# Cross-attention with a state-space scan: the last query block in two halves, the scan begun in the pipeline's drain and the last 256 steps scanned on their own

## The chip, the cores and the metric

The kernel runs on one core of a Trainium2 chip. Its engines are PE (TensorE: matmul, with weight loads shown as PEld), DVE (VectorE), ACT (ScalarE), POOL (GpSimd) and SP (SyncE, used here as the main DMA queue). The metric is the device time of one execution in microseconds; the median of the runs shown is 2639.42 us.

## The reference

`x` (4096 x 512) gives the queries and the residual, `ctx` (3202 x 512) the keys and values; there are 8 heads of 64, and the state has 64 entries.

```python
x = _layernorm(builder_state, g1, beta1)
base_n = _layernorm(base_state, g1, beta1)
x = residual + _mha(x, base_n, W_qkv, b_qkv, W_o, b_o)
residual = x
xn = _layernorm(x, g2, beta2)
U = (xn @ W_in.T + b_in) @ Bmat

def step(s, u_t):
    s = jax.nn.silu(s @ A.T) + u_t
    return (s, s)
_, states = jax.lax.scan(step, jnp.zeros((builder_state.shape[0], S), U.dtype), U.transpose(1, 0, 2))
ssm_out = jnp.einsum('tbs,sh->bth', states, Cmat)
x = residual + ssm_out
mod = program_probs.mean(axis=1) @ W_prog.T + b_prog
return x + mod[:, None, :]
```

The scan runs one step after another along the 4096 positions. The mean of a second context gives `mod`, one row for all. Everything is in f32.

## The kernel before

**Preparation (to about 300 us).** The context is normalised, transposed and projected; keys and values are written to DRAM (`kd`, `vd`) as 13 double chunks of up to 248 keys for each pair of heads. Constants are folded: `rowb` (the attention's output bias), `modb` (the program bias), `wc`, `bu`, and `a_t`, the transposed state matrix twice on a 128x128 diagonal, so that two halves of the sequence run on 128 partitions.

**The attention loop.** The 4096 queries are 8 blocks Q of 512. A unit is (Q, hp, half): one pair of heads and 256 queries; units run with `half` innermost, so one load of keys and values (`load_k`, `load_v`, four steps ahead, 13 buffers each) serves two units. A unit has 13 steps, one for each double chunk. The whole order is written out by hand: iteration g of one loop (L721) issues, for every engine, `running` of step g-1 (DVE maximum, L480), `weights` of step g-17 (ACT exp, L524, and POOL's accumulation `acc`, L533, a tile of 123x1024), `scores` of step g (PE, L459, and ACT's copy to SBUF, L469), `subtract` of step g-16 (DVE, L514) and `product` of step g-18 (PE, L542). The exact maximum of a unit is known only after all its scores (`maximum`), hence the distance of 16 steps; each engine carries out its own instructions in the order in which they are issued. After the last scores the loop goes on for 18 iterations with subtractions, exps and products alone: this is called the drain below. For the very last unit every second accumulation is done on PE instead (`sums`, L558).

One generator at a time is advanced beside the steps by `background`: `finish` (divides a unit's output by the sum of its weights), `queries` (normalises and projects the next block) and `project` (for each tile of 128 rows of a finished block: output projection L627, residual, second normalisation, transposes L136, then `u` through `wc`, L659 and L663, and the row itself to DRAM, `x1d`, L648). Tiles of the loop write x1 without `modb`; the adds of `modb` come later, as rows are fetched back (L784).

**After the loop (L768 on).** The pools are released. The four tiles of the last block run through `project` together, as the scheduler orders them; the rows of all blocks are fetched back from `x1d` in the scan's layout, row = (v, c, j): v one of two halves of the sequence (on partitions 0 to 63 and 64 to 127), c one of 128 chunks in it, j one of 16 positions in a chunk.

**The scan.** The recurrence forgets its start quickly, so 256 chunks of 16 steps run side by side: sweep a does the last 8 positions of each chunk from no state, sweep b all 16 from what a left in the chunk before, sweep c 16 more from b, with outputs. One step is a matmul with `a_half` on h (L853), a tanh (L857) and one DVE operation (L858, h = (tanh + 1) z); the matmul of `a_t` on u was put into the same PSUM bank ahead (L840, L845). `output` adds u (L864), multiplies by `c2` (L870, two matmuls of 512 columns), adds the row (L873) and writes it from ACT's queue (L874). A final check compares the ends of sweeps b and c within 2^-21; if one differs, a sequential loop under `tc.If` repeats the work (L905).

```python
            nc.scalar.activation(th, zj, AF.Tanh, scale=0.5)
            nc.vector.scalar_tensor_tensor(h[:, j, :], th, 1.0, zj, ALU.add, ALU.mult)
```

Of the kernel before, what the change touches and what calls it, by code (L numbers as in the profile page):

```python
# [31 lines left out]
WARM = 8  # L32
NCK = T // L // 2
# [12 lines left out]
def xattn_ssm_kernel(  # L46
# [30 lines left out]

    u = const.tile([P, L, NCK], F32, name="u")

# [159 lines left out]
    def side():  # L239
# [75 lines left out]
        yield  # L315
        mean = wp.tile([NS, 1], F32, name="mean")
# [116 lines left out]
    lctx = ExitStack()  # L433
# [132 lines left out]
    def finish_last(w):  # L566
        Q, hp, half = w["at"]
        o = o_t[Q, hp][:, half * QU : (half + 1) * QU]
        nc.scalar.copy(o, w["po"][:, 0, :])
        sums(w["pd"], w["acc"], CK, False, True)  # L570
        rd = op.tile([P, QU], F32, tag="rd", name="rd_last", bufs=1)
# [4 lines left out]
        nc.vector.tensor_tensor(o, o, rd, ALU.mult)  # L576

    def finish(w):
# [3 lines left out]
        if half == 0:  # L582
            o_t[Q, hp] = op.tile([P, QB], F32, tag="o", name=f"o_{Q}_{hp}")
        o = o_t[Q, hp][:, half * QU : (half + 1) * QU]
# [31 lines left out]
    def project(Q, tiles=range(NT), pools=None):  # L616

        xp, n_x, n_t = pools or (xp_, 3, 1)
        for t in tiles:
            r = Q * QB + t * P  # L620
            xt = xp.tile([P, H], F32, tag="x", name=f"xr_{r}", bufs=n_x)
# [4 lines left out]
            for c in range(NC):  # L626
                nc.tensor.matmul(  # L627
                    pa,
                    o_t[Q, c][:, t * P : (t + 1) * P],
# [5 lines left out]
            x1 = xp.tile([P, H], F32, tag="x1", name=f"x1_{r}")  # L635
            nc.vector.tensor_tensor(x1, pa, xt, ALU.add)  # L636
            scaled = normalize(x1, P, f"y{r}", later=True)
            xs = x1
            if Q == NQB - 1:

                nc.gpsimd.tensor_tensor(xt, x1, modb, ALU.add)
                xs = xt
# [5 lines left out]
            nc.sync.dma_start(x1d[r : r + P, :], xs)  # L648
            tp = transposes(ps_m, "m", xh, P, f"y{r}")
            yield True  # L650
            xn = xp.tile([P, NC, P], F32, tag="xn2", name=f"xn2_{r}", bufs=n_t)
# [6 lines left out]
            for c in range(NC):  # L658
# [8 lines left out]
                None,  # L667
                ALU.add,
            )
# [4 lines left out]
    def load_k(i, c):  # L674

        Q, hp, half = units[i]
        if half == 0:
            t = kp.tile([P, 2 * CK], F32, tag="k", name=f"k_{Q}_{hp}_{c}")
            n = 2 * keys(2 * c)
            nc.sync.dma_start(t[:, :n], kd[hp, c, :, :n])  # L680
            kts[Q, hp, c] = t

    def load_v(i, c):
        Q, hp, half = units[i]
        if half == 0:
            t = kp.tile([CK, 2, P], F32, tag="v", name=f"v_{Q}_{hp}_{c}")
# [5 lines left out]
    units = [(Q, hp, half) for Q in range(NQB) for hp in range(NC) for half in range(2)]  # L692
# [24 lines left out]

    with tc.manual_schedule():
        for g in range(AHEAD):
            load_k(*steps[g])  # L720
        for g in range(len(steps) + NDC + LAG + 2):  # L721
# [22 lines left out]
            if exp:  # L744
                weights(*exp)
            if now:
# [5 lines left out]
            if mul:  # L752
                product(*mul)
                if mul[0]["last"] and mul[1] == NDC - 1:
                    finish_last(mul[0])
# [42 lines left out]

# [163 lines left out]
```

## Time and profile before

| | us |
|---|---|
| median of 3 runs | 2639.42 |
| lowest and highest run | 2634.09, 2639.81 |
| profiled execution, its time | 2643.8 |
| its span | 2642.0 |
| busy in the span: PE, DVE, ACT, POOL | 2498.9, 2144.1, 1837.8, 2066.3 |
| mean granted PE clock | 0.981 |
| last running maximum starts | 2468.65 |
| last sum of weights ends on PE | 2498.75 |
| first matmul of sweep a | 2545.02 |
| sweep c's first state on DVE | 2583.71 |
| end of the span | 2642.0 |

The profile's rows give, for a group of instructions: start, busy time, engine, line, operation, output and inputs with their shapes and the count; in brackets, how long the engine had been idle and what ended that. Windows give the busy time of every engine between two points in time, the mean clock granted to PE, and what the DMA engines did. One execution is profiled, and its time is 4.4 us above the median of the runs.

### The profile page before, as it was taken

What the parts mean: (1) busy time and instruction counts of PE and PEld (TensorE: products, weight loads), DVE (VectorE), ACT (ScalarE), POOL (GpSimd) and SP (SyncE); (2) the same over time, 40 slices, a digit from 0 to 9 for tenths busy, and PEclk for the clock granted to TensorE, in tenths of its full rate; (3) what the DMA queues carried; (4) which work ended last, traced back from release to release, by engine and by line L of the source; (5) the groups of instructions that cost most, each with busy time, mean ns of one, the idle gap of its engine ahead of it and who ended that gap; (6) DMA issues with size and microseconds to landing.
All of it is one profiled execution on the core that took longest, in us unless ns stands there. A gap on an engine that the chain in (4) does not pass through costs nothing.

```text
span 2642.0 us, 44166 instructions
## 1 busy us (share of the span) xinstructions
PE 2498.9 (95%) x16588; PEld 1422.2 (54%) x16588; DVE 2144.1 (81%) x2320; ACT 1837.8 (70%) x2085; POOL 2066.3 (78%) x1170
## 2 busy tenths in 40 slices
PE   7989899999999999999999999999999999999857
PEld 3445456555565555555655555555655555555433
DVE  2210897999979897999799988999799979999725
ACT  2232787877878787878787777778787878788510
POOL 1020497998979997999799988989799979999860
PEclk9999999999999999999999999999999999999966
DMA  3422221112212121222112211222121312221133
GB/s 124 138 87 73 74 68 49 51 57 84 59 45 62 50 83 32 58 65 68 45 54 68 67 56 51 57 84 59 43 62 49 86 30 60 64 58 54 60 112 128
DMA packets 164458, 176.62 MB, mean 67 GB/s; under 512 B 13480, under 2 KB 137424, under 8 KB 164242
## 3 DMA queue, kind: packets, MB, share of 16 engines
q1 hardware_dynamic: 155070, 157.68, 20.6%
q10 hardware_dynamic: 9172, 16.06, 1.8%
q8 instruction: 134, 2.20, 0.4%
q14 instruction: 82, 0.67, 0.1%
HBM read 143.81 MB, written 29.89 MB: 66 GB/s over the span
## 4 chain that ended last, share of the span: by engine, by line
PE 50%; DVE 27%; issue 11%; ACT 7%; POOL 2%; DMA 1%; SPq 1%; ACTq 0%; DVEq 0%; POOLq 0%
DVE top L480 17%; PE s L459 14%; PE po L542 12%; DVE p L514 5%; PE pq L175 4%; ACT p L469 4%; PE pa L627 4%; PE pv L388 3%; PE pk L414 3%; ACT p L524 2%; PE tt L491 2%; PE py_c L870 1%; DVE rd L599 1%; PE mb L506 1%; PE pu L659 1%
## 5 line engine op out<-in xcount | busy, mean ns | idle before, releaser
L533 POOL TENSOR_TENSOR acc<-p,acc 123x1024 f32<-123x1024 f32 x698 | 1658.7, 2376 | 112.2 <-ACT p L524 70.6
L469 ACT COPY p<-s 123x1024 f32<-123x1024 f32 (+1 forms) x832 | 834.9, 1004 | 274.6 <-PE s L459 261.9
L514 DVE TENSOR_TENSOR p<-p,mb 123x1024 f32<-123x1024 f32 (+1 forms) x832 | 1000.0, 1209 | 0.8 <-PE mb L506 0.8
L459 PE MATMUL s<-q,k 64*123 64x256 f32 (+1 forms) x6656 | 941.4, 402 | 61.2 <-DVE top L480 49.4
L524 ACT ACTIVATE p<-p 123x1024 f32<-123x1024 f32 (+1 forms) x832 | 880.2, 1058 | 141.2 <-DVE p L514 134.0
L480 DVE TENSOR_TENSOR top<-s,top 123x1024 f32<-123x1024 f32 x704 | 855.9, 1216 | 140.1 <-ACT p L469 132.2
L542 PE MATMUL po<-p,v 123*64 123x256 f32 (+1 forms) x6656 | 900.4, 392 | 1.1 <-ACT o L585 0.9
L459 PEld LDWEIGHTS s<-q,k 64*123 64x123 f32 (+1 forms) x6656 | 560.2, 182 | 374.3 <-DVE top L480 169.3
L542 PEld LDWEIGHTS po<-p,v 123*64 123x64 f32 (+1 forms) x6656 | 404.4, 136 | 399.0 <-issue 222.5
L533 POOL TENSOR_TENSOR acc<-p,p 124x1024 f32<-124x1024 f32 x64 | 152.0, 2376 | 161.2 <-ACT p L524 161.0
L627 PE MATMUL pa<-wo,o 128*128 128x512 f32 x256 | 119.6, 612 | 2.5 <-DVE x L636 2.5
L115 POOL TENSOR_SCALAR ve_c<-mv_c 123x1 f32<-123x1 f32 (+1 forms) x26 | 5.9, 228 | 146.9 <-DVE mv_c L113 116.7
L175 PE MATMUL pq<-xn,wq 128*128 128x256 f32 x512 | 117.9, 383 | 0.0
L358 DVE COPY ct<-tp_c 128x492 f32<-128x492 f32 (+1 forms) x13 | 8.7, 671 | 127.8 <-PE tp_c L136 127.8
L480 DVE TENSOR_TENSOR top<-s,p 124x1024 f32<-124x1024 f32 x64 | 77.7, 1214 | 38.7 <-DMA k<-kd 37.4
L175 PEld LDWEIGHTS pq<-xn,wq 128*128 128x128 f32 x512 | 94.8, 190 | 20.5 <-issue 6.3
L388 PE MATMUL pv<-wv,ct 128*123 128x512 f32 (+1 forms) x208 | 97.8, 615 | 0.0
L422 ACT ACTIVATE ks<-pk,bias 128x492 f32<-128x492 f32 (+2 forms) x28 | 18.0, 643 | 111.8 <-PE pk L414 63.6
L414 PE MATMUL pk<-ct,wk 128*128 128x492 f32 (+2 forms) x224 | 89.2, 550 | 0.0
L588 POOL TENSOR_TENSOR both<-acc 124x512 f32<-124x512 f32 x63 | 80.8, 1283 | 4.9
L627 PEld LDWEIGHTS pa<-wo,o 128*128 128x128 f32 x256 | 46.8, 192 | 62.5 <-issue 56.5
L498 DVE TENSOR_REDUCE m<-tt 128x2 f32<-128x496 f32 x128 | 79.7, 662 | 0.7 <-PE tt L491 0.7
(158 smaller groups left out, 1345.5 us busy)
## 6 DMA issues: line engine op xcount, KB each, us to landing
k<-kd SPq DMA_DIRECT2D x352, 123.0 KB
v<-vd SPq DMA_DIRECT2D x352, 123.0 KB
xr<-in_x_dram SPq DMA_DIRECT2D x32, 256.0 KB
out_dram<-row_c ACTq DMA_DIRECT2D x32, 256.0 KB
k<-kd SPq DMA_DIRECT2D x64, 124.0 KB
v<-vd SPq DMA_DIRECT2D x64, 124.0 KB
x<-in_x_dram SPq DMA_DIRECT2D x28, 256.0 KB
x1d<-x SPq DMA_DIRECT2D x28, 256.0 KB
```

What stands on the lines that cost most here:

```text
L175: nc.tensor.matmul(pq[:, half * QU : (half + 1) * QU], wq[:, i, hp * P : (hp + 1) * P], xns[half][:, i, :], start=(i == 0), stop=(i == NC ...
L388: nc.tensor.matmul(pv[:n, :H], ct[:, i, o : o + n], wv[:, i, :], start=(i == 0), stop=(i == NC - 1),)
L414: nc.tensor.matmul(pk[:, :n_g], wk[:, i, hp * P : (hp + 1) * P], ct[:, i, :n_g], start=(i == 0), stop=(i == NC - 1),)
L459: nc.tensor.matmul(s[:n, a, b, :], kts[(*w["at"][:2], c)][r, b * n : (b + 1) * n], q[r], start=True, stop=True,)
L469: nc.scalar.copy(t[:n], s[:n])
L480: nc.vector.tensor_tensor(w["top"][:n], s[:n], before[:n], ALU.max)
L514: nc.vector.tensor_tensor(t[:n], t[:n], w["mb"][:n].unsqueeze(2).to_broadcast([n, 2, 2, QU]), ALU.subtract,)
L524: nc.scalar.activation(t[:n], t[:n], AF.Exp)
L533: nc.gpsimd.tensor_tensor(w["acc"][:n], t[:n], before[:n], ALU.add)
L542: nc.tensor.matmul(w["po"][a * HD : (a + 1) * HD, 0, :], vts[(*w["at"][:2], c)][:n, b, a * HD : (a + 1) * HD], t[:n, a, b, :], start=(c == ...
L588: nc.gpsimd.tensor_tensor(both, acc[:, :, 0, :], acc[:, :, 1, :], ALU.add)
L627: nc.tensor.matmul(pa, o_t[Q, c][:, t * P : (t + 1) * P], wo[:, c, :], start=(c == 0), stop=(c == NC - 1),)
```

## The change

Four things change.

1. **The last block by halves.** Its units run with `half` outermost: all four head pairs for queries 3584 to 3839, then all four for the last 256. Keys and values are loaded again for the second half. The first half's two tiles go through `project` in the loop's background.
2. **The row adds.** Every tile now gets `modb` on POOL in `project`, before it is written to `x1d`; the adds at the fetch are gone.
3. **The scan of the first 3840 positions** (`main_scan`) starts in the drain: 12 of its steps are issued in iterations 1 to 8, 10, 12, 14 and 16 after the last scores, between ACT's exp and DVE's subtraction. Its steps hold the state s = h + u instead of h, so that a step is one matmul, a tanh and two DVE operations, and nothing is put into PSUM ahead. Rows are fetched from SP's queue during the drain. The rest of the scan is issued alternately with the last two tiles and the small scan; of an output's two halves, one goes over ACT and POOL, the other over DVE, and both are written from SP's queue.
4. **The last 256 positions** (`last_rows`) have a scan of their own: two tiles on the two halves of the partitions, 16 chunks of 8 positions each, with 24 positions of warm-up and 8 of result, 32 steps in a row on 16 columns. A second check compares their starts.

`a_t` is halved and `u` is doubled; the columns of `u` that belong to the last 256 positions are zeroed.

```diff
+LT = 8
+PRE = 3 * LT
...
+    END = NCK - QU // L
+    nc.gpsimd.memset(u[NS:, :, END:], 0.0)
...
+        nc.vector.tensor_scalar(a_t, a_t, 0.5, None, ALU.mult)
...
     def finish_last(w):
         Q, hp, half = w["at"]
-        o = o_t[Q, hp][:, half * QU : (half + 1) * QU]
+        o = op.tile([P, QU], F32, tag="o", name=f"o_{Q}_{hp}_{half}", bufs=12)
+        o_t[Q, hp, half] = o
         nc.scalar.copy(o, w["po"][:, 0, :])
         sums(w["pd"], w["acc"], CK, False, True)
+        yield
...
-    def project(Q, tiles=range(NT), pools=None):
-        xp, n_x, n_t = pools or (xp_, 3, 1)
+    def project(Q, tiles=range(NT), wait=0):
+        for _ in range(wait):
+            yield False
...
-            xs = x1
-            if Q == NQB - 1:
-                nc.gpsimd.tensor_tensor(xt, x1, modb, ALU.add)
-                xs = xt
+            nc.gpsimd.tensor_tensor(xt, x1, modb, ALU.add)
...
-            nc.sync.dma_start(x1d[r : r + P, :], xs)
+            nc.sync.dma_start(x1d[r : r + P, :], xt)
...
     def load_k(i, c):
         Q, hp, half = units[i]
-        if half == 0:
-            t = kp.tile([P, 2 * CK], F32, tag="k", name=f"k_{Q}_{hp}_{c}")
+        if half == 0 or Q == NQB - 1:
+            t = kp.tile([P, 2 * CK], F32, tag="k", name=f"k_{Q}_{hp}_{half}_{c}")
...
-    units = [(Q, hp, half) for Q in range(NQB) for hp in range(NC) for half in range(2)]
+    units = [(Q, hp, half) for Q in range(NQB - 1) for hp in range(NC) for half in range(2)]
+    units += [(NQB - 1, hp, half) for half in range(2) for hp in range(NC)]
...
+    def fetch(j):
+        if j not in rows:
+            rows[j] = sp_.tile([P, 2, H], F32, tag="s", name=f"row_{j}")
+        for v, n in enumerate(counts):
+            nc.sync.dma_start(rows[j][:n, v, :], x1r[v, j, :n])
+    def last_fetch():
+        for g in range(2):
+            r = LAST + g * P
+            t = xp_.tile([P, H], F32, tag="x", name=f"xr_{r}", bufs=3)
+            nc.sync.dma_start(t, x[r : r + P, :])
+            xl.append(t)
...
+        for g in range(2):
+            nc.gpsimd.tensor_tensor(xl[g], xl[g], rowb, ALU.add)
+    def step(j, before, s, z):
+        nc.tensor.matmul(z, a_t, before, start=True, stop=True)
+        th, h = sv["th"][j % 2], sv["h"][j % 2]
+        nc.scalar.activation(th, z, AF.Tanh, scale=0.5)
+        nc.vector.scalar_tensor_tensor(h, th, 1.0, z, ALU.add, ALU.mult)
+        nc.vector.tensor_tensor(s, h, u[:, j, :], ALU.add)
...
+    def sweep(first, start, end):
+        before = start
+        for j in range(first, L):
+            s = end[:, 1:] if j == L - 1 else sv["s"][j % 3]
+            step(j, before, s, zs(j))
+            before = s
+            yield j, s
+        nc.vector.tensor_copy(end[NS:, 0:1], end[:NS, NCK : NCK + 1])
+    def products(j, s):
+        for v, n in enumerate(counts):
+            r = slice(v * NS, (v + 1) * NS)
+            nc.tensor.matmul(sv["py"][j % 2][v], s[r, :], sv["c2"][r], start=True, stop=True)
+    def outputs(j):
+        py, t, y = sv["py"][j % 2], rows[j], sv["y"][:, j % 2, :]
+        nc.scalar.activation(y, py[1], AF.Copy, scale=0.5)
+        nc.vector.scalar_tensor_tensor(
+            t[:, 0, :], py[0], 0.5, t[:, 0, :], ALU.mult, ALU.add
+        )
+        n = counts[1]
+        nc.gpsimd.tensor_tensor(t[:n, 1, :], y[:n], t[:n, 1, :], ALU.add)
+        for v, n in enumerate(counts):
+            nc.sync.dma_start(outr[v, j], t[:n, v, :]) if n == NCK else nc.sync.dma_start(
+                outr[v, j, :n], t[:n, v, :]
+            )
...
+    def main_scan():
+        ends = sv["end0"], sv["end1"]
+        sv["z"] = ps_s.tile([P, 2, 4, NCK], F32, tag="s", name="z")
+        for end in ends:
+            nc.vector.memset(end[:NS, 0:1], 0.0)
...
+        for _ in sweep(L - WARM, u[:, L - WARM - 1, :], ends[0]):
+            yield
+        for _ in sweep(0, ends[0][:, :NCK], ends[1]):
+            yield
+        for j, s in sweep(0, ends[1][:, :NCK], ends[0]):
+            yield
+            products(j, s)
+            outputs(j)
+            yield
+        differ(ends[0][:, 1:], ends[1][:, 1:], NCK, sv["bad"])
+        yield
+    def last_rows(w):
+        yield from finish_last(w)
+        Q, tiles = NQB - 1, range(2)
+        pas, x1s, scaled, xns = [], [], [], []
+        for g in tiles:
+            pa = ps_m.tile([P, H], F32, tag="m", name=f"pa_l{g}")
+            pas.append(pa)
+            for c in range(NC):
+                nc.tensor.matmul(
+                    pa, o_t[Q, c, 1][:, g * P : (g + 1) * P], wo[:, c, :],
+                    start=(c == 0), stop=(c == NC - 1),
+                )
+            yield
+        for g in tiles:
+            x1 = xp_.tile([P, H], F32, tag="x1", name=f"x1_l{g}")
+            x1s.append(x1)
+            nc.vector.tensor_tensor(x1, pas[g], xl[g], ALU.add)
+            scaled.append(normalize(x1, P, f"yl{g}", later=True))
+            yield
+        tps = []
+        for g in tiles:
+            xh = scaled[g]()
+            tps.append(transposes(ps_m, "m", xh, P, f"yl{g}"))
+            nc.gpsimd.tensor_tensor(xl[g], x1s[g], modb, ALU.add)
+            yield
...
+        for g in tiles:
+            xn = sv["xn"][:, g, :].rearrange("p (c k) -> p c k", c=NC)
+            nc.scalar.copy(xn, tps[g])
...
+        for i in range(PRE // LT + 1):
+            nc.tensor.matmul(
+                zl[:, i, :], a_t, ul[:, i * LT : i * LT + P], start=(i == 0), stop=True,
+                skip_group_check=True,
+            )
+        yield
+        before = None
+        for t in range(PRE + LT):
+            i, j = divmod(t, LT)
+            z = zl[:, i, j::LT]
+            if before is not None:
+                nc.tensor.matmul(z, a_t, before, start=False, stop=True, skip_group_check=True)
+            h = (hl if i == PRE // LT else hw)[:, j::LT]
+            nc.scalar.activation(th, z, AF.Tanh, scale=0.5)
+            nc.vector.scalar_tensor_tensor(h, th, 1.0, z, ALU.add, ALU.mult)
+            if t == PRE:
+                nc.vector.tensor_tensor(sv["st"], hw[:, LT - 1 :: LT], ul[:, PRE :: LT][:, : P // LT], ALU.add)
+            before = h
+            yield
+        nc.vector.tensor_tensor(sl[:, 1:], hl, ul[:, PRE + 1 :], ALU.add)
+    def last_outputs(name):
+        sl = sv["sl"]
+        for g in range(2):
+            hs = slice(g * NS, (g + 1) * NS)
+            py = ps_m.tile([P, H], F32, tag="m", name=f"py_{name}_{g}")
+            sv["pyl", g] = py
+            nc.tensor.matmul(py, sl[hs, 1:], sv["c2"][hs], start=True, stop=True)
+        for g, queue in enumerate((nc.sync, nc.scalar)):
+            nc.vector.scalar_tensor_tensor(
+                xl[g], sv["pyl", g], 0.5, xl[g], ALU.mult, ALU.add
+            )
+            queue.dma_start(out[LAST + g * P : LAST + (g + 1) * P, :], xl[g])
...
+    SCAN_AT = (*range(1, 9), 10, 12, 14, 16)
+    scan = main_scan()
...
+            k = g - len(steps)
+            if k == 0:
+                assert not rest
+                last_fetch()
+            if k in SCAN_AT:
+                next(scan)
...
-                if mul[0]["last"] and mul[1] == NDC - 1:
-                    finish_last(mul[0])
-                elif mul[1] == NDC - 1:
+                if mul[1] == NDC - 1 and not mul[0]["last"]:
                     first.append(finish(mul[0]))
-                    if mul[0]["at"][1:] == (NC - 1, 1):
+                    if mul[0]["at"] == (NQB - 1, NC - 1, 0):
+                        rest.append(project(NQB - 1, range(NT // 2), wait=8))
+                    elif mul[0]["at"][1:] == (NC - 1, 1):
                         rest.insert(0, project(mul[0]["at"][0]))
+            if 0 < k <= L:
+                fetch(k - 1)
...
-        while first or rest:
-            background()
-    lctx.close()
...
-    def fetch(v, j, c0, c1, name):
...
-    tails = [project(NQB - 1, (t,), (tp_, NT, NT)) for t in range(NT)]
-    for g in tails:
-        next(g)
-    for j in range(L):
-        fetch(0, j, 0, NCK, "c")
-        fetch(1, j, 0, done, "c")
-    while tails:
-        for g in list(tails):
-            if next(g, None) is None:
-                tails.remove(g)
-    for j in range(L):
-        fetch(1, j, done, NCK, "c")
...
+        end = last_rows(ws[len(units) - 1])
+        next(end)
+        for _ in end:
+            next(scan, None)
+        for _ in scan:
+            pass
+        last_outputs("a")
+        neighbours()
+        differ(sv["sl"][:, : P : LT], sv["st"], P // LT, sv["badl"])
...
```

## The prediction

> **What bounds the kernel now.** I read the stages first (busy time of each engine in windows), then the count of steps in the last block, the timeline of the tail, and the granted clock inside it. Columns after the window: length, then busy PE, PEld, DVE, ACT, POOL with counts, clock, DMA share, GB/s.
>
> ```profile
> 2468.65:2498.75 30.10, 24.64 (x213) 15.10 (x211) 22.20 (x28) 18.62 (x20) 27.05 (x12) 1.00 0.01 2
> 2498.75:2545.02 46.27, 25.41 (x80) 14.35 (x80) 10.26 (x20) 5.48 (x8) 42.53 (x44) 0.74 0.80 231
> 2545.02:2582.67 37.65, 25.00 (x68) 13.99 (x69) 9.11 (x29) 6.66 (x24) 10.69 (x9) 0.70 0.01 2
> 2582.67:2636.40 53.73, 46.92 (x99) 19.09 (x97) 31.06 (x70) 4.44 (x16) 0.00 (x0) 0.61 0.39 147
> 2636.40:2642.00 5.60, 0.19 (x2) 0.09 (x2) 1.63 (x8) 0.00 (x0) 0.00 (x0) 0.68 0.29 102
> ```
> From the last running maximum on, 173.35 us: drain 30.1, four last tiles 46.3, sweeps a and b 37.7, sweep c with outputs 53.7, end 5.6. No engine is full there except PE in sweep c; they are chains. Before it, the block's loop, by windows of ACT's copies of scores (one per step) and of all engines:
>
> ```profile
> 2158.00:2250.00 92.00, 39.01 (x39) 1.00 0.20 56
> 2250.00:2346.00 96.00, 33.82 (x34) 1.00 0.25 73
> 2346.00:2466.00 120.00, 50.19 (x51) 1.00 0.15 42
> ...
> 2250.00:2346.00 96.00, 96.00 (x666) 54.33 (x664) 88.20 (x94) 72.80 (x81) 86.20 (x50) 1.00 0.25 73
> 2346.00:2466.00 120.00, 115.87 (x882) 65.82 (x880) 119.08 (x118) 100.96 (x109) 115.00 (x52) 1.00 0.15 42
> ```
> A plain step costs 212/90 = 2.36 us, and DVE is full (119.08 of 120); with four tiles of a projection inside, PE is full and 34 steps take 96 us, so a tile costs (96 - 34 x 2.36)/4 = 4.0 us. POOL has 9.8 us spare there.
>
> **The change, part by part.** What is removed is the whole of the stages after the drain (143.25 us); what replaces it is summed below, stage by stage. The zeroing of u's end and the halving of a_t are one short instruction each beside the first 300 us of preparation: nothing.
>
> Loop. Two tiles move into it: +8.0. Their POOL adds of modb, and those of the 28 earlier tiles, are new there: 30 x 1.265 us. Below, 0 (POOL has 9.8 us spare per four tiles for 5.1); above, all 38. I take 2: DVE has waited for POOL's rowb add, 16.8 us over 18 tiles, so cover is not complete. The write of a tile to DRAM now waits for that add; behind it on SP stand key and value loads, some nine steps (21 us) early, so 4 us later hurts nobody. Reloaded keys and values (104 DMAs of 123 KB) run at the rate that every second unit has now; their buffers are free nine (keys) and seven (values) steps before. Nothing; without that cover, the landing of a load per step. Sum +10.
>
> Drain. It gets twelve scan steps. Order matters: in an iteration ACT runs exp, then the scan's tanh; DVE runs the scan's two operations, then the next subtraction; that exp waits for the subtraction before it. So these iterations are one ring: subtraction 1.21 + exp 1.06 + tanh 0.28 + 2 x 0.29 + four hand-overs of 0.03 = 3.25 us, where DVE now needs 1.21. PE's products stand behind a scan matmul that waits for DVE, but within the ring. First three iterations: 7.8 us to the first subtraction of the last unit, plus three shortened rings, 11.4. That holds the scan's setup copies too. Then five rings 16.3, one bare 1.2, three (ring + bare) 13.4, reduction and reciprocal 1.2, last exp, product and sums 3.0: 46.5. The 32 row loads now stand on SP among the value loads: 7.9 MB in some 50 us (158 GB/s; 311 were moved between 2500 and 2520). Each waits for a buffer that the product one step before frees, and the value loads behind have five steps to spare: nothing, or one step's 3.25 us if a load came late.
>
> The step's last operation adds two SBUF tensors, and POOL is adding accumulators beside it (27.05 of 30.1 us). The trace has no such DVE operation beside POOL; it has copies of 128x127:
>
> ```profile
> 2536.11 19.60 POOL L784 TENSOR_TENSOR row_c<-row_c,modb 128x512 f32<-128x512 f32 x16
> 2545.00 1.01 DVE L820 COPY us<-u 128x127 f32<-128x127 f32 x1
> 2555.12 0.67 DVE L828 COPY he<-h 128x127 f32<-128x127 f32 x1
> 2580.72 0.23 DVE L828 COPY he<-h 128x127 f32<-128x127 f32 x1
> ```
> 0.23 us without POOL; with it the second copy ends 0.08 us after POOL's last add (2555.71). So it waited for the running add. Bounds per step: 0 (the subtraction with one SBUF input runs at 1.21 beside POOL throughout) and one whole accumulator add, 2.38. I follow the copies: half an add, 1.2. POOL's work here, 27.05 + 2 x 1.27 for the rows, fills 0.6 of 50 us: 12 x 0.6 x 1.2 = 8.6. Drain 55.1, between 46.5 and 75.
>
> The Trainium skill (SBUF — State Buffer, Who interferes with whom) speaks against the change here: a VectorE tensor-tensor with both inputs in SBUF contends with GpSimd's reads, and whichever comes second is blocked for the whole instruction. By the page the sum is as above; if only copies were blocked, it would be 8.6 less, and no run here shows the tensor-tensor yet.
>
> Last two tiles. Ten scan steps run between them in program order. At full clock: reciprocals and scaling 2.5; two projections (1.85 + scan matmul 0.5) 4.7; twice add, statistics and the scan's DVE pair (1.56 + 0.62) 4.4; twice normalise 0.81, transposes 0.66, scan matmul to its end 1.45: 5.8; twice copy 0.59, four matmuls 1.0, scan 1.45: 6.1; u and the four matmuls of the small scan 2.6; 26. At half clock behind the projections about 32. Taken: 30.
>
> Scan steps and outputs. The rows for a step, at both clocks:
>
> ```profile
> 2549.20 0.49 PE L853 MATMUL z_a<-h,a_half 128*128 128x128 f32 x2 [0.69 <-DVE h L858]
> 2549.72 0.28 ACT L857 ACTIVATE th_a<-z_a 128x128 f32<-128x128 f32 x1 [0.90 <-PE z_a L853]
> 2550.03 0.29 DVE L858 SCALAR_TENSOR_TENSOR h<-th_a,z_a 128x128 f32<-128x128 f32 x1 [0.89 <-ACT th_a L857]
> ...
> 2584.78 4.93 PE L870 MATMUL py_c<-c,st_c 64*128 64x512 f32 x8
> ...
> 2604.82 3.10 PE L870 MATMUL py_c<-c,st_c 64*128 64x512 f32 x8
> ```
> A step now takes 1.17 us (1.48 at half clock); the added DVE operation makes it 1.5 (1.8). The first two small steps go beside two of these: 2 x (1.8 + 0.35) = 4.3. Then fifteen pairs: one main step, its products, two small steps. Chain: small matmul 0.3 (0.43; its row is the 128-wide one, less the time of 112 columns), main step 1.5 (1.8), products 1.55 (2.46): 3.4 (4.7). POOL's output add (1.27) starts 0.6 after the products and overlaps the two-input add: +0.45 at full clock, about 0.05 at half. So 3.85 (4.75). Clock: sweep c now stands at 0.61, that is full for a quarter of it. Pairs: 0.25 x 3.85 + 0.75 x 4.75 = 4.5, x15 = 68.
>
> ```profile
> 2583.00:2599.00 16.00, 14.50 (x28) 5.97 (x28) 8.24 (x18) 1.39 (x5) 0.00 (x0) 0.50 0.33 124
> 2600.00:2612.00 12.00, 9.75 (x29) 3.71 (x28) 8.39 (x19) 1.12 (x5) 0.00 (x0) 0.93 0.48 177
> 2612.50:2632.00 19.50, 17.25 (x34) 7.16 (x34) 10.55 (x23) 1.66 (x6) 0.00 (x0) 0.50 0.43 161
> ```
> PE is 88 to 91% busy at half clock and stays there, with no idle stretch above 1.5 us. The Trainium skill (TensorE: Matmul & The Clock Gate, HAM oscillation) has it that the clock falls for idle gaps of some 3.4 us and rises on as much sustained work. By that rule the pairs would be at full clock, 15 x 3.85 = 58, ten less; the rows disagree, and I go by them.
>
> End. Sixteenth step and products 4.3, last two products 2.46, add 0.7, copies and second check 1.8, count 0.5, and 3.5 from the count to the end as now: 13.2. The row writes move from ACT's queue to SP's, behind nothing late.
>
> Sum: 10 + 55.1 + 30 + 4.3 + 68 + 13.2 = 180.6 against 173.35: +7. The profiled run took 2643.8 us (span 2642.0); the median shown is 2639.4, 0.2% less. The difference goes on the median: 2646.5.
>
> **Rivals.** (1) Not slower: the clock. If the denser PE order of the tail (by the chain above some 0.6 us idle per pair of 4.7, against 1.5 in 7.1 now) holds the full clock, pairs are 58 and the tiles 24: -16, so 2631. It decides from about 0.55 of the time at full clock. For it: 2600 to 2612. Against: the two stretches at 0.50.
> (2) The two-input add does not wait for POOL: -8.6 in the drain, -2 in the pairs: 2636. For it: the subtraction. Against: the copies.
> (3) POOL becomes the loop's bound: at 60% of its 38 us exposed, +21 beyond the 2 taken: 2667. For it: 115 of 120 us busy in plain stretches. Against: the spare 9.8, and the wait for POOL's reductions on PE is 1.9 us in 660.
> (4) It does not do what it says: a check of the last 256 steps fails and the fallback loop runs, thousands of us. Warm-up is 24 steps, as before; 0.01.
>
> **Numbers.** Forecast 0.41, (1) 0.28, (2) 0.14, (3) 0.16, (4) 0.01. What a measurement can tell from no change is about 0.2%, 5.3 us. The forecast's own range is 2638 to 2655: slower 0.31, same 0.10. (1) faster 0.26, same 0.02; (2) faster 0.05, same 0.09; (3) and (4) slower. Together faster 0.31, same 0.21, slower 0.48. Range 2620 to 2666: it leaves out the full clock without any wait for POOL below, and the worse half of a bound POOL above.
>
> **What would show it.** Rings of 3.2 us between exps in the drain; the scan's adds of h and u longer than 0.29 us where POOL runs; two-step pairs of 4.7 at clock 0.5; u of the first half's tiles written inside the loop. It is wrong if the drain stays below 45 us, or sweep c runs at clock 1.00.

## The result and the profile after

| | before | after |
|---|---|---|
| median of the runs, us | 2639.07 (2634.09 to 2639.81, 4) | 2653.81 (2651.83 to 2654.75, 4) |
| profiled execution: time / span, us | 2643.8 / 2642.0 | 2654.64 / 2652.9 |
| mean granted TensorE clock | 0.981 | 0.973 |

The kernel became slower: the ratio is 1.0059, with an interval of 1.0042 to 1.0076. Forecast were 2646.5 us and slower; the time is 7.3 us above the number and inside the range.

The loop first. Three rows of each kernel's timeline (start, duration, engine, line, tiles): the first running maximum over 124 keys after 300 us, the last scaling of a query projection, and the last running maximum. Before:

```profile
322.14 1.21 DVE L480 TENSOR_TENSOR top<-s,p 124x1024 f32<-124x1024 f32 x1
...
2156.81 0.69 ACT L184 ACTIVATE q<-pq,bias 128x512 f32<-128x512 f32 x1
...
2468.65 1.22 DVE L480 TENSOR_TENSOR top<-s,top 123x1024 f32<-123x1024 f32 x1
```
After:

```profile
324.45 1.21 DVE L485 TENSOR_TENSOR top<-s,p 124x1024 f32<-124x1024 f32 x1
...
2159.53 0.69 ACT L188 ACTIVATE q<-pq,bias 128x512 f32<-128x512 f32 x1
...
2479.91 1.21 DVE L485 TENSOR_TENSOR top<-s,top 123x1024 f32<-123x1024 f32 x1
```
The last running maximum starts 11.26 us later, but 2.31 of that is there at the first row already. The later runs, whose code up to that row is this kernel's, have it anywhere from 319.5 to 325.3, so this part lies within the scatter of that stretch. From the first row on, the query projection comes 0.41 us later than before and the end of the loop 8.95 us. So the part of the loop up to there, with POOL's new additions for the earlier blocks' tiles, costs 0.4 us, and the rest, with two more tiles, 8.5.

The tail, as stages of windows (start and end, length, busy PE, PEld, DVE, ACT, POOL with counts, clock, DMA share, GB/s), after:

```profile
2479.91:2534.95 55.04, 38.44 (x237) 21.11 (x236) 40.07 (x52) 21.22 (x32) 29.27 (x14) 0.81 0.56 166
2534.95:2563.22 28.27, 19.80 (x67) 13.15 (x68) 11.83 (x30) 4.84 (x13) 4.61 (x8) 0.69 0.05 19
2563.22:2568.34 5.12, 2.49 (x10) 1.98 (x9) 2.02 (x9) 1.20 (x6) 0.00 (x0) 0.50 0.00 0
2568.34:2634.08 65.74, 56.20 (x149) 28.68 (x149) 23.89 (x75) 16.33 (x58) 17.70 (x14) 0.50 0.31 105
2634.08:2652.90 18.82, 4.95 (x16) 1.85 (x14) 8.84 (x29) 1.47 (x3) 2.53 (x2) 0.59 0.24 83
```
The stages are the drain (from the last running maximum to the first reciprocal of the last unit), the last two tiles (to the end of the small scan's four products), the first two small steps, fifteen pairs, and the end from the sixteenth step on. They are the terms of the prediction's sum (of the small scan's 32 steps three, not two, fall into the third stage: ACT's tanh at 2563.85, 2565.73 and 2567.54):

| term, us | predicted | measured |
|---|---|---|
| loop, added | 10 | 9.0 |
| drain | 55.1 | 55.0 |
| last two tiles | 30 | 28.3 |
| first two small steps | 4.3 | 5.1 |
| fifteen pairs | 68 | 65.7 |
| end | 13.2 | 18.8 |
| sum, against 173.35 | 180.6 | 181.9 |

The change took 143.25 us of stages away and put 118 in their place, but the drain grew by 24.9 and the loop by 9. The drain's timeline, after (in brackets the idle time before an instruction and what ended it):

```profile
2482.30 2.04 DVE L836 COPY scan<-u 64x9 f32<-64x9 f32 x1
...
2486.80 7.20 POOL L538 TENSOR_TENSOR acc<-p,acc 123x1024 f32<-123x1024 f32 x3
...
2489.36 2.36 DVE L782 TENSOR_TENSOR scan<-scan,u 128x128 f32<-128x128 f32 x1
...
2503.13 1.06 ACT L529 ACTIVATE p<-p 123x1024 f32<-123x1024 f32 x1 [3.57 <-DVE p L519]
...
2504.78 0.29 DVE L782 TENSOR_TENSOR scan<-scan,u 128x128 f32<-128x128 f32 x1
...
2506.23 1.06 ACT L529 ACTIVATE p<-p 123x1024 f32<-123x1024 f32 x1 [1.88 <-DVE p L519]
2507.43 2.35 POOL L538 TENSOR_TENSOR acc<-p,acc 123x1024 f32<-123x1024 f32 x1 [5.61 <-ACT p L529]
...
2507.88 2.05 DVE L782 TENSOR_TENSOR scan<-scan,u 128x128 f32<-128x128 f32 x1
```
Two things are to be seen. The exponentials at 2503.13 and 2506.23 stand 3.10 us apart with an addition of 0.29 between them: the ring, worked out as 3.25. And the addition of two SBUF tensors takes 0.29 us at 2504.78, where POOL is idle, but 2.36 and 2.05 inside a running POOL addition. The twelve additions of the drain took 0.93, 2.36, 0.90, 0.29, 1.98, 0.29, 2.05, 0.29, 0.82, 1.01, 1.01 and 0.93 us: 9.4 above twelve times 0.29.

### The profile page after: what moved, and what is told of

It reads as the page before. It is cut to its first block, busy times and chain, and to the rows that moved or that the text cites. A ratio compares the mean times of both kernels' runs of the same rounds, so it can differ in the third digit from the quotient of the medians.

```text
span 2652.9 us, 44604 instructions
## 1 busy us (share of the span) xinstructions
PE 2511.1 (95%) x16642; PEld 1433.9 (54%) x16642; DVE 2161.1 (81%) x2372; ACT 1849.0 (70%) x2133; POOL 2073.8 (78%) x1183
## 4 chain that ended last, share of the span: by engine, by line
PE 50%; DVE 28%; issue 11%; ACT 8%; DMA 1%; SPq 1%; POOL 0%; ACTq 0%; DVEq 0%
DVE top L485 17%; PE s L464 15%; PE po L547 13%; DVE p L519 6%; PE pq L179 4%; PE pa L635 4%; ACT p L474 4%; PE pv L393 3%; PE pk L419 3%; ACT p L529 2%; PE tt L496 2%; DVE rd L606 1%; PE mb L511 1%; PE pu L664 1%; DVE m L503 1%
## 5 line engine op out<-in xcount | busy, mean ns | idle before, releaser
L635 PE MATMUL pa<-wo,o 128*128 128x512 f32 x240 | 111.0, 605 | 0.0
L810 POOL TENSOR_TENSOR row<-y_l,row 112x512 f32<-112x512 f32 x16 | 20.2, 1264 | 69.7 <-ACT scan L912 40.8
```

The costliest lines, as they stand in the source:

```text
L635: nc.tensor.matmul(pa, o_t[Q, c, t // 2][:, t % 2 * P : (t % 2 + 1) * P], wo[:, c, :], start=(c == 0), stop=(c == NC - 1),)
```

## Experiments on the drain

The ratio is to the kernel before the change on the same chip; stages are from each run's profile, divided as above.

| run | median us | ratio (95%) | drain | pairs | end |
|---|---|---|---|---|---|
| after | 2653.81 | 1.0059 (1.0042 to 1.0076) | 55.0 | 65.7 | 18.8 |
| e1_port | 2641.03 | 1.0007 (0.9996 to 1.0018) | 46.7 | 64.8 | 16.6 |
| e2_order | 2640.48 | 1.0006 (0.9996 to 1.0016) | 43.3 | 65.7 | 18.8 |
| e3_both | 2641.15 | 1.0008 (0.9998 to 1.0017) | 45.4 | 64.8 | 18.5 |
| e4_none | 2658.88 | 1.0072 (1.0052 to 1.0092) | 38.2 | 66.3 | 18.1 |
| e6_rows | 2634.46 | 0.9984 (0.9974 to 0.9995) | 38.9 | 64.8 | 18.1 |
| e9_nomodb | 2652.38 | 1.0053 (1.0033 to 1.0073) | 55.0 | 65.7 | 19.6 |

**The wait for POOL (e1_port).**

```diff
-        nc.vector.scalar_tensor_tensor(h, th, 1.0, z, ALU.add, ALU.mult)
-        nc.vector.tensor_tensor(s, h, u[:, j, :], ALU.add)
+        nc.vector.scalar_tensor_tensor(z, th, 1.0, z, ALU.add, ALU.mult)
+        nc.vector.tensor_tensor(s, z, u[:, j, :], ALU.add)
```


> The scan step's product (th+1)z is written back over z in PSUM, so the step's last operation adds one PSUM and one SBUF tensor in place of two from SBUF. Theory A (the drain's 55.0 us are a ring of subtraction, exponential, tanh and the scan's two operations, some 46, plus about 9.4 us in which the adds with two SBUF inputs wait for POOL): every add of the main scan takes about 0.3 us, the drain falls by 8 to 10 to 45 to 47, the time is 2643 to 2647. Rival B (the drain is set by PE at half clock and by the 32 row loads on SP, and the long adds lie beside that): the adds are short, but the drain stays above 52 and the time above 2651. Rival C (the wait for POOL is not tied to two SBUF inputs): the adds stay at up to 2.4 us and nothing changes.

The addition's rows in the drain (durations are least, median and greatest, in ns), first in the changed kernel, for ten of the twelve additions, then in this run for all twelve:

```profile
L782 DVE TENSOR_TENSOR scan<-scan,u x10: 292/916/2361, 2484.8 to 2522.8; 128x128 f32<-128x128 f32 x10
```
```profile
L782 DVE TENSOR_TENSOR scan<-z,u x12: 291/292/295, 2481.8 to 2521.2; 128x128 f32<-128x128 f32 x12
```
With one operand in PSUM no addition waits. The drain falls by 8.3 us to 46.7, which is the bare ring of the prediction, 46.5. Theory A holds; B and C fall. Two things came along with it. The time fell by 12.8 us, below the 2643 to 2647 expected; 2.2 of that lie between the count and the end of the span (6.1 us in the changed kernel, 3.9 here). And the drain's mean granted clock rose from 0.81 to 0.93; how much of the 8.3 us is TensorE's, these runs don't separate. The prediction weighed the Trainium skill's page "SBUF — State Buffer" (Who interferes with whom), by which a VectorE tensor-tensor with both inputs in SBUF and a GpSimd read block each other for a whole instruction. This pair of runs agrees: 916 ns in the median with two SBUF inputs, 292 with one, and at 2489.36 a whole 2.36 us.

**The order (e2_order), and both edits (e3_both).**

```diff
-            if k in SCAN_AT:
-                next(scan)
 ...
             if 3 not in ends and sub:
                 subtract(*sub)
+            if k in SCAN_AT:
+                next(scan)
```


> In each drain iteration the scan step is issued behind the subtraction and not ahead of it; nothing else changes. Theory A: the next exponential no longer waits for the scan's tanh and its two DVE operations, so an iteration with a scan step falls from some 3.3 us and the wait for POOL to about 2.4 us and the wait; drain 43 to 48, time 2643 to 2648; adds still up to 2.4 us. Rival B (PE's clock or the row loads set the drain): drain above 52, time above 2651.

> Both edits together: product written back into PSUM, and the scan step behind the subtraction. Theory A: ring and wait for POOL are separate terms that add, drain 36 to 40, time 2635 to 2640, no slower than the kernel before the change (2639). If the two terms are one (the same idle time removed twice): drain 43 to 47, time 2643 to 2647. Rival B: drain above 52.

The order alone gives 11.7 us of drain, so the ring is real as well. The wait for POOL was not gone by it: six of the drain's twelve additions still took 0.71 to 1.98 us (0.93, 1.06, 0.92, 0.71, 1.98, 1.72), 5.6 us above twelve times 0.29 against 9.4:

```profile
L782 DVE TENSOR_TENSOR scan<-scan,u x12: 291/505/1975, 2480.7 to 2515.6; 128x128 f32<-128x128 f32 x12
```
Both edits together gave no more, and the drain was even 2.1 us longer, in the range that was written down for "the two terms are one". The three medians, 2640.5 to 2641.2, can't be told apart. The timeline of the run with both edits says what ended the wait now, and it is neither term:

```profile
2507.91 12.73 SPq L745 DMA_DIRECT2D row<-x1d  x12
...
2510.00 1.08 PE L547 MATMUL po<-p,v 123*64 123x256 f32 x8 [1.07 <-DMA v<-vd]
...
2514.21 1.13 PE L547 MATMUL po<-p,v 123*64 123x256 f32 x8 [1.84 <-DMA v<-vd]
...
2517.71 1.98 PE L547 MATMUL po<-p,v 123*64 123x256 f32 x8 [2.37 <-DMA v<-vd]
```
The last three products of the drain wait 5.3 us for value loads that stand on SP among the 32 row loads. The prediction had costed the row loads at nothing and named their cover, value loads five steps early. In the kernel as changed the slow ring kept that cover; with a shorter ring it is gone.

**The row loads behind the drain (e6_rows).** On top of e3_both:

```diff
-            if 0 < k <= L:
-                fetch(k - 1)
 ...
         assert not first and not rest
+        for j in range(L):
+            fetch(j)
```


> On top of both edits to the drain (product written back into PSUM, scan step behind the subtraction) the 32 row loads are issued behind the drain's last value load and not two per iteration among them. Theory A' (with the shorter ring the row loads take the DMA queue's rate, and the drain's last three products wait for value loads that come late, some 5.3 us of waits and half a clock after them): no product of the drain waits for a value load, drain 36 to 40 against 45.4, time 2632 to 2637. Rival B (the late values only fill a gap that something else, PE at half clock, would leave): waits for values gone, drain 43 to 46, time as with the two edits, 2639 to 2643. Rival D (the rows then come too late for the outputs): drain short, but the pairs grow by as much.

No product waits for a value load, the drain is 38.9, in the 36 to 40 forecast for two separate terms, and the pairs did not grow. So the terms are not one; of 8.3 and 11.7 us won alone, 16.1 are won together. This kernel does what the changed one does and is a little faster than the kernel before, 0.9984 (0.9974 to 0.9995), though by less than the 0.2% that the prediction held could be told from no change.

**No scan in the drain (e4_none).**

```diff
-    SCAN_AT = (*range(1, 9), 10, 12, 14, 16)
+    SCAN_AT = ()
```


> No scan step runs in the drain; the 12 steps run beside the last two tiles and the last 256 steps instead. Theory A: the drain falls to 31 to 35 (before the change: 30.1), and the twelve steps cost 18 to 24 in the tail behind it, so the time is 2648 to 2656: the steps in the drain gain next to nothing. Rival B (32 row loads and PE's clock set the drain): it stays above 45 without any scan step, and the time is above 2660.

This was half a miss: the steps cost what was expected, but drain and time lie above their ranges. The drain fell only to 38.2, with a late value load in it even without a scan step:

```profile
2515.03 1.08 PE L547 MATMUL po<-p,v 123*64 123x256 f32 x8 [2.89 <-DMA v<-vd]
```
Besides, POOL's two additions of `rowb` to the last rows (2.50 us at 2484.16) now stand ahead of its accumulations, and TensorE waits 4.2 us for `both` where it waited 2.0 before the change. The two waits would make some 5 of the 8.1 us by which this drain is longer than before the change. The twelve steps cost 22.6 us beside the small scan, and the time was 2658.9. So a step cost 1.41 us in the changed drain (16.9 by 12) and 1.9 behind it. Moving the scan there was worth some 5 us (5.1 by the medians); how the step was built, ordered and fed gave away 16 (drain 38.9 in e6_rows).

**POOL's additions (e9_nomodb).**

```diff
-            nc.gpsimd.tensor_tensor(xt, x1, modb, ALU.add)
 ...
-            nc.sync.dma_start(x1d[r : r + P, :], xt)
+            nc.sync.dma_start(x1d[r : r + P, :], x1)
```


> The changed kernel without POOL's addition of modb to the 30 tiles that the loop projects; the program bias is left out of these rows' residual. Counted from the first running maximum over 124 keys after 300 us, the changed kernel's last query projection comes 0.4 us later than before the change and its last running maximum 9.0 to 9.2 us. My theory (two tiles at 4.0 to 4.4, the additions next to nothing): the last running maximum still comes 8.0 to 9.0 us later than before. Rival (3) of the prediction in a weak form (POOL's additions make half or more of the 9): it comes 4.5 us later or less.

From the same first row (321.24 here) the last query projection comes after 1835.1 us and the last running maximum after 2155.5; with the additions these are 1835.1 and 2155.5. They cost nothing. Nor do the reloaded keys and values, as far as the waits tell: from 2160 to 2480 us of the changed kernel TensorE's products wait for no load, only 3.8 us for the running maximum. That leaves 8.5 of the loop's 9.0 to the two tiles, some 4.3 each.

## Experiments on the end and on the clock

**The end (e8_end), on top of e6_rows.**

```diff
             products(j, s)
+            if j == L - 1:
+                differ(ends[0][:, 1:], ends[1][:, 1:], NCK, sv["bad"])
             outputs(j)
             yield
-        differ(ends[0][:, 1:], ends[1][:, 1:], NCK, sv["bad"])
 ...
-        last_outputs("a")
+        last = last_outputs("a")
+        next(last)
         neighbours()
 ...
         nc.vector.tensor_copy(nbad, pbad[0:1, 0:1])
+        for _ in last:
+            pass
```
Here `last_outputs` stops between its products and its additions, and the count goes to the scan's z, so that it needs no buffer of the last outputs.

> The kernel with the row loads behind the drain, and the end put in another order: the main check is issued ahead of the sixteenth step's output operations, the last two output products ahead of the second check, their additions and writes behind the count. Theory A' (the end's 17.4 us from the last addition of the small scan are a chain on DVE: wait behind POOL, main check, last outputs, second check, count, and 3.5 to 6 us from the count to the end): end 12.5 to 15, time 3 to 5 us under the kernel without this edit, 2628 to 2634, ratio to before 0.996 to 0.998. Rival (the last writes' landing sets the end, not the count): end stays at 16.5 to 17.5.

The end fell from 18.1 to 15.6 (16.7 to 14.2 as the expectation counts it, from the last addition of the small scan), the time to 2631.70, ratio 0.9974 (0.9963 to 0.9984), 2.8 us under e6_rows where 3 to 5 were expected. The chain on DVE was a part of it. From the count to the end of the span there were 6.8 us here and 5.2 in e6_rows. Kernels with the same end differ in it too, 3.9 in e1_port, 5.8 in e3_both, 6.1 in the changed kernel, 6.9 in e9_nomodb; what sets it stays open.

**The clock: products that nothing reads.** `fill` is a PSUM tile of its own. Ahead of a step's output products:

```diff
+            if j == 0:
+                sv["f"] = ps_m.tile([P, H], F32, tag="m", name="fill")
+            for _ in range(2):
+                nc.tensor.matmul(sv["f"], a_t, sv["c2"], start=True, stop=True)
             products(j, s)
```
Two in each step are e7_fill (on e6_rows). e12_fill64 is the same with the first 64 rows alone (`a_t[:NS]`, `sv["c2"][:NS]`). On e8_end, one in each step is e10_fill1, two in the first step alone e11_burst, and two in steps 0, 4, 8 and 12 e13_every4.

> The kernel with the row loads behind the drain, and in each of the sixteen output steps two more TensorE products of 128 rows by 512 columns into a tile that nothing reads, issued ahead of the output products, so that TensorE has no idle time there. Rival (1) of the prediction in its strong form (the granted clock follows how dense TensorE's order is): the clock of the pairs goes to 0.9 or more and a pair takes 3.4 to 3.9 us against 4.4. My theory (it stays at 0.50 at 85 to 91% busy, and density is not what is missing): clock 0.50, a pair takes 5.7 to 6.4 us, the time grows by 20 to 30 us.

My expectation failed outright. By windows of the run with two products per step:

```profile
2549.00:2556.00 7.00, 6.75 (x16) 3.06 (x16) 0.84 (x5) 0.82 (x3) 0.00 (x0) 0.57 0.01 2
2556.00:2562.00 6.00, 4.75 (x19) 2.25 (x18) 2.92 (x10) 1.75 (x8) 2.18 (x2) 1.00 0.25 88
...
2570.00:2621.00 51.00, 43.73 (x156) 19.32 (x156) 17.61 (x57) 11.67 (x46) 14.41 (x12) 1.00 0.31 106
```
Within the first step the clock went to 1.00 and stayed. TensorE is 86% busy there (43.73 of 51), about as much as at 0.50 in the changed kernel (56.20 of 65.74, 85%): the busy share does not tell the two apart. Sixteen times two extra products (1.96 us a pair at full clock) made the pairs 70.6 us and the time only 4.65 us longer than e6_rows, 2639.11 (ratio 1.0003, 0.9990 to 1.0016). The other four:

| run | median us | ratio (95%) | pairs |
|---|---|---|---|
| e12_fill64 | 2661.24 | 1.0082 (1.0065 to 1.0100) | 93.7 |
| e11_burst | 2628.81 | 0.9963 (0.9949 to 0.9977) | 59.9 |
| e10_fill1 | 2625.00 | 0.9944 (0.9930 to 0.9957) | 61.3 |
| e13_every4 | 2635.22 | 0.9967 (0.9952 to 0.9982) | 62.0 |

> The kernel with the row loads behind the drain, and two products per step as in the run with two of 128 rows, but of 64 rows each: TensorE is as long busy, with half of its rows. If what counts is only that TensorE has an instruction running, the clock is 1.00 as there, a pair 4.6 us, time 2636 to 2642. If what counts is how much of the array works, the clock stays at 0.50, a pair takes 5.7 to 7.5 us and the time is 2655 to 2680.

```profile
2557.00:2562.00 5.00, 5.00 (x10) 1.89 (x9) 0.28 (x1) 0.24 (x1) 0.00 (x0) 0.50 0.17 52
...
2592.00:2597.00 5.00, 4.06 (x14) 1.82 (x11) 1.45 (x5) 1.03 (x4) 1.27 (x1) 0.88 0.37 122
```
With 64 rows the clock was 0.50 while TensorE was busy all of 5.00 us, and 0.65 over the stage's 94 us. So a running instruction is not enough. But the stretches at 0.88 are not what half the array alone would give, so the second reading is not shown clean.

> The kernel with the new end, and two products of 128 rows by 512 columns that nothing reads ahead of the first step's output products alone; the other fifteen steps have none. Theory G (it is the missing unbroken stretch alone: once the clock is up, it falls only for idle gaps of several us, and the pairs have none above 1.5 us): clock 1.00 from the second pair to the last, a pair 3.4 to 3.9 us, the pairs 53 to 58, time 2618 to 2624. Theory E (density has to last): the clock is up for some 10 to 16 us after the burst, as in the stretch of 12 us at 0.93 before the change, and falls again; the pairs 62 to 67, time 2628 to 2633.

```profile
2547.00:2552.00 5.00, 5.00 (x14) 1.91 (x13) 0.68 (x3) 0.66 (x3) 0.00 (x0) 0.67 0.01 3
2552.00:2557.00 5.00, 3.29 (x17) 1.91 (x18) 3.10 (x10) 1.92 (x8) 2.53 (x2) 1.00 0.40 141
...
2562.00:2567.00 5.00, 3.61 (x16) 1.75 (x16) 2.20 (x8) 1.23 (x5) 2.31 (x2) 1.00 0.45 158
2567.00:2572.00 5.00, 4.50 (x16) 2.58 (x14) 1.81 (x6) 1.80 (x6) 1.38 (x2) 0.54 0.40 137
2572.00:2577.00 5.00, 4.58 (x14) 2.43 (x12) 2.40 (x8) 1.41 (x5) 1.98 (x2) 0.50 0.29 101
```
After one burst the clock stood at 1.00 for some 17 us, and four steps took 12.21 us (output additions at 2552.39 and 2564.60): 3.05 each, against 4.38 in the changed kernel. Then it fell for the rest of the pairs, as theory E had it; their 59.9 us lie between the ranges of E and G, and they are those of the fastest of the five executions (2622.95 us). TensorE's longest idle time in those 17 us was 0.92 us, and the fall shows in the length of the scan's own product, 0.47 us until then:

```profile
2565.43 0.40 PE L915 MATMUL zl<-scan,a_t 128*128 128x16 f32 x2 [0.92 <-DVE scan L918]
...
2567.25 0.67 PE L778 MATMUL z<-scan,a_t 128*128 128x128 f32 x2
```
The prediction set the Trainium skill's rule against the rows ("TensorE: Matmul & The Clock Gate", What's actually happening and HAM oscillation: the clock falls for idle gaps of some 3.4 us and rises on as much sustained work). The fall does not agree: no gap here came near 3.4 us. The rise agrees in this run, 3.56 us of unbroken products and then the full clock, but not in general. In sweep c of the kernel before the change:

```profile
2591.18:2600.83 9.65, 9.65 (x20) 4.30 (x21) 4.68 (x11) 0.83 (x3) 0.00 (x0) 0.50 0.36 136
2615.95:2622.39 6.44, 6.44 (x12) 2.62 (x12) 3.46 (x7) 0.28 (x1) 0.00 (x0) 0.50 0.37 138
```
TensorE had no gap in either window, and the clock was 0.50. It rose behind the first alone, which holds the only product of 128 rows by 512 columns from 2583 to 2632:

```profile
2597.35 1.91 PE L840 MATMUL z_c<-u,a_t 128*128 128x512 f32 x2
```
So the record of before held a hint that such products count for more than 64-row ones. How they are counted, these runs don't tell.

> The kernel with the new end, and one TensorE product of 128 rows by 512 columns that nothing reads ahead of each of the sixteen steps' output products (two of them: pairs at clock 1.00 from the second on, a pair 4.6 us, of which the two take 1.96). Theory E (TensorE's clock rises after an unbroken stretch of work and holds while its order has few gaps; one product fills the wait for the step's state): clock 1.00 from the first pairs on, a pair 3.5 to 3.9 us, the pairs 54 to 60 against 66.1, time 2620 to 2626, ratio to before 0.992 to 0.995. Rival F (one is not enough to raise the clock): clock 0.50, a pair 5 to 5.7 us, time 2640 to 2652.

```profile
2550.60:2567.00 16.40, 15.44 (x34) 5.88 (x33) 4.21 (x14) 3.20 (x12) 2.98 (x3) 0.55 0.17 60
2567.00:2611.00 44.00, 36.42 (x143) 16.12 (x144) 18.48 (x61) 11.84 (x46) 14.73 (x12) 1.00 0.39 134
```
One product per step holds the clock for the 44 us that are left, at 3.73 us a step, but needs three steps to raise it. So the pairs are 61.3, above the 54 to 60, and the time is within the 2620 to 2626. It has the lowest median of all that ran, 0.9944 of the kernel before. TensorE is 83% busy while the clock holds (36.42 of 44); in e11_burst it was 70% busy at 1.00 (10.46 of 15.00 us from 2552 to 2567), and there the clock fell. That may be the reason, but no run isolates it.

> The kernel with the new end, and two products of 128 rows by 512 columns that nothing reads ahead of every fourth step's output products (0, 4, 8, 12). With the burst in the first step alone the clock stood at 1.00 for some 17 us, five steps of 3.05 us, and then at 0.50, 4.3 us a step. If a burst every four steps holds the clock: 1.00 from the second step to the last, steps of 3.05 and of some 4.6 us where a burst stands, the pairs 51 to 55 against 61.3, time 2616 to 2624, ratio to before 0.990 to 0.994. If the clock falls at a time of its own, whatever the bursts do, and a burst at half clock raises it again only late: a mixture, the pairs 58 to 64, time 2624 to 2632.

The pairs, 62.0, are the mixture of the second theory (the time lies above its 2632, where the kernel before took 2642.4 in the same runs). The burst in the fifth step did not keep the clock up:

```profile
2568.50 1.96 PE L847 MATMUL fill<-c,a_t 128*128 128x512 f32 x4
```
```profile
2569.00:2574.00 5.00, 3.94 (x16) 1.88 (x16) 1.54 (x6) 1.03 (x4) 1.52 (x2) 0.96 0.29 99
2574.00:2579.00 5.00, 4.42 (x14) 2.08 (x12) 1.55 (x5) 1.13 (x4) 1.26 (x1) 0.50 0.46 157
```
Two of the twelve executions, 2622.8 and 2623.0 us at a mean clock of 0.990 against 0.985 in the profiled one, lie in the first theory's range; no trace shows what the clock did in them. Two in the first step and one in every other would join what e11_burst and e10_fill1 showed; it was not tried.

## Why the prediction was right, point by point

**Loop.** Right in size, 9.0 for 10. The mechanism of the tiles held (some 4.3 us each for 4.0; `u` of the first half's tiles is written at 2435.1 and 2460.0, inside the loop); the 2 us for POOL's additions were not there. Rival (3) falls, by e9_nomodb.

**Drain.** Right, 55.0 for 55.1, and both parts are shown one by one: the bare ring 46.7 for 46.5 (e1_port), and the wait for POOL 8.3 for 8.6 by its removal, 9.4 by the durations. Rival (2) falls. The sum took TensorE at full speed, though, and the granted clock was 0.81. The two parts do not quite add either: 8.3 and 11.7 us alone are 16.1 together. What the prediction called nothing, the row loads, was nothing only behind a slow drain.

**Tiles and small steps.** 33.4 for 34.3, with three small steps where the sum had two.

**Pairs.** 65.7 for 68, by two misses that partly cancel, which is luck. The clock was 0.50 throughout where a quarter at full speed was assumed. And the output products were cheaper than the row they were priced by:

```profile
2630.07 0.78 PE L778 MATMUL z<-scan,a_t 128*128 128x128 f32 x2
...
2632.07 2.08 PE L800 MATMUL py<-c,scan 64*128 64x512 f32 x4 [0.68 <-DVE scan L913]
...
2636.91 1.22 PE L800 MATMUL py_b<-c,scan 64*128 64x512 f32 x1 [2.04 <-DVE scan L782]
...
2636.92 1.22 PE L800 MATMUL py_o<-c,scan 64*128 64x512 f32 x1
```
Four passes over two times 64 rows take 2.08 us at half clock, not the 2.46 (half of 4.93), and the rows at 2636.91 and 2636.92 show two of the passes starting together on the two halves of the rows (one pass of a product takes 1.22 us there). A pair took 4.38 us, not 4.75.

**End.** The step that failed: 18.8 for 13.2. The sum had "last two products 2.46, add 0.7, copies and second check 1.8, count 0.5", and left out that the main check stands ahead of them on DVE:

```profile
2639.91 0.28 DVE L819 TENSOR_REDUCE scan<-scan 128x1 f32<-128x128 f32 x1
...
2640.30 0.91 DVE L821 TENSOR_TENSOR scan<-scan 128x128 f32<-128x128 f32 x1
...
2642.91 1.29 DVE L929 SCALAR_TENSOR_TENSOR xr<-py_a,xr 128x512 f32<-128x512 f32 x2
...
2646.22 0.15 DVE L827 TENSOR_SCALAR scan<-scan 128x1 f32<-128x1 f32 x1
...
2646.66 0.15 DVE L1026 CAST nbad<-pbad 1x1 int32<-1x1 f32 x1 [0.28 <-PE pbad L1022]
```
The main check runs from 2639.91 to 2642.95, 3.0 us (its subtraction again waits for POOL, 0.91). The last two products run beside it, from 2638.78, so in place of their 2.46 the chain has 3.9 us on DVE, an output addition and the check: 1.4 more. The sixteenth step, the last additions and the second check took 4.9, 1.3 and 2.2 us for 4.3, 0.7 and 1.8: 1.7 more. And from the count to the end there were 6.1 us, 2.6 more than the 3.5 taken from before; as said, this stretch differs between executions. Together, with 0.1 less for the count, that is the 5.6. Against it stand the pairs, 2.3 under their term, the tiles and the loop: that the sum came out within 1.3 us is luck in part.

**Rival (1), the clock.** It did not happen, and its price was not wrong: the pairs stood at 0.50, but a denser order does bring the full clock (e7_fill, e10_fill1), and without products that nothing reads a step then takes 3.05 us (e11_burst). The prediction held that the clock "stays there" at 88 to 91% busy. It does as long as nothing raises it; the rows shown then did not tell that a burst of 3.6 us would.

**The rest of the 7.3 us.** The stages explain 1.3 (181.9 for 180.6) and the scatter ahead of the first row 2.3. The other 3.7 lie nearly all in how the profiled executions stand to the medians: before, the profiled one took 4.4 us more than the median that the prediction added its 7 to; after, 0.8.

## What to carry to other kernels

Work that is moved beside a drain must not stand in the drain's way: put it behind the instruction that releases the next long one, keep one operand of a VectorE addition in PSUM where POOL is adding, and keep bulk loads off the queue that feeds the drain. Remove such terms one at a time and look at what ends the wait next; here the second edit bought nothing until the row loads had moved too. In a long tail of dependent products read the granted clock before the busy share: a product that nothing reads, in a wait that is there anyway, made the kernel faster (0.9974 of the kernel before without it, 0.9944 with it).

## What the runs showed of the hardware that was not expected

- TensorE at 85% busy stood at clock 0.50 for 65.7 us; at 86% with 128-row products in its gaps it stood at 1.00 for 51 us. After a burst of 3.56 us it was at 1.00 for some 17 us and fell with no idle time above 0.92 us. Products of 64 rows, back to back, left it at 0.50 for whole windows, and 9.65 us without a gap before the change passed at 0.50.
- Two products of 64 rows by 512 columns on different halves of the rows run at the same time: their first passes start within 0.01 us and take 1.22 us at half clock, and all four passes take 2.08 us.
- The first 320 us end anywhere between 319.5 and 325.3 us in profiled executions of kernels with the same code up to there, more than the 0.2% by which kernels are told apart.
